# A two-matrix macaron block with an S4 convolution: the second half of the convolution by pairs of blocks, and a rewritten opening

## The chip, the cores and the metric

The kernel runs on one core of one Trainium2 chip. The metric is device time in microseconds for one launch. A NeuronCore has TensorE (PE; its weight loads are listed apart as PEld), VectorE (DVE), ScalarE (ACT), GpSimd (POOL) and SyncE (SP), which here only issues DMAs.

## The reference

The input `u` is 2 x 1024 x 1024 in float32. With LN a layer norm without weights, three residual steps follow each other:

```
x = u
x = x + 0.5 * FFN(LN(x))
x = x + S4(LN(x))
x = x + 0.5 * FFN(LN(x))          # the same weights as in the first FFN

FFN(x) = (silu(x @ Wg) * (x @ Wu)) @ Wd        # 1024 -> 2752 -> 1024
W[k, n] = scales[k // 128, n] * (w4[k, n] - (z4[k // 128, n] + 1))   # 4 bits, packed by 8 in int32

S4(u):  K = ifft of a rational function of 64 poles at 1024 roots of unity
        y = irfft(rfft(u, 2048) * rfft(K, 2048))[..., :1024]      # causal convolution along the last axis
        return y + D * u
```

The convolution runs along the last axis, 1024 long, and is the same for each of the 2048 rows. It is therefore a product with a Toeplitz matrix: output column m gets the sum over n <= m of u[n] K[m - n]. Cut into 8 x 8 blocks of 128, the block that takes input block c to output block m depends on m - c alone and is zero for m < c.

## The kernel before

**Tiling.** The 2048 rows are four token blocks of 512 (`TB`), each four tiles of 128 (`NT`). `JOBS` lists eight jobs (block, step): each is one feed-forward pass over one block, in the order (0,1), (1,1), (0,3), (1,3), (2,1), (3,1), (2,3), (3,3). Step 3 is the second FFN. A job has two stages, `gate_up` and `down`.

**gate_up** has 64 steps: eight waves of two or three pairs of 128 columns, and in each wave the eight groups of 128 input rows. In a step every unit of 128 columns gets two products of 512 columns, with the low and the high part of the normalized and turned input (`pieces`; L501). Between groups the partial sum in PSUM is multiplied by the ratio of two scales (`scaled`; L477 on ACT, L479 on DVE), so the weights themselves stay small integers. On the last group of a wave `gated` makes silu(gate) * up (L523, L526) and splits it into a high and a low part on GpSimd (L528, L530). `acc` has six PSUM banks for the six units. **down** has 44 steps, 22 for each half of the output, with products at L562 and the same rescales.

**Weights.** Job 0 also makes the weights. `fetch` and `fetch_zeros` load packed words and zero points, `split` separates even and odd nibbles (L381, L382), `dequantize` subtracts (L396) and writes the result to a DRAM buffer `w_q` (L400); `load_w` reads tiles back (L461), `AHEAD` = 3 steps early, from a pool of six buffers that `dequantize` shares. The first tile of all is put together in SBUF by eight small DMAs on ACT's queue (L399). `zero_points` makes the table of zero points and writes it to DRAM, from where `fetch_zeros` spreads it over partitions.

**Order.** The work around the matmuls hangs on steps: `at(up, s, f)` and `at(dn, s, f)` run `f` when step `s` of a stage is written. The program's framework then orders the instructions of each engine by when it expects them to be ready and, among ready ones, by the order of writing; so an instruction can come earlier on its engine than it was written. It also inserts the waits.

**The opening**, before the first step: zero points, loads of x, `moments` (bn_stats, L137) and `deviations` (1/sqrt by Newton steps on tiny tiles), `less_mean` (L1173), the eight `dequantize` of wave 0, the first scales, the multiplication by 1/deviation (L1185), and `turn` (transposes L173, high part L187, low part L188). Second halves of x are turned in steps 0 to 3.

**The convolution.** Between step 1 and step 3 of a block, in jobs 1, 2, 5 and 6, each of its four token tiles is normalized, turned (`turn_whole`; tile `st`) and convolved (`convolve`; products L835 into `pc`, adds L843). `toeplitz` holds the 8 different Toeplitz blocks, 128 x 1024, made in job 1 by `s4_tables`. `bank` hands out the two PSUM banks of the pool `ps`. The products are in float32: each shows as two matmul and two weight-load instructions.

Of the kernel before, what the change touches and what calls it, by code (L numbers as in the profile page):

```python
# [9 lines left out]
F32 = mybir.dt.float32  # L10
# [6 lines left out]
AX = mybir.AxisListType  # L17
PSUM = bass.MemoryType.PSUM
DRAM = bass.MemoryType.DRAM

P = 128
# [28 lines left out]
def macaron_s4_kernel(  # L50
# [64 lines left out]


# [52 lines left out]
    def turned(n, half, name, bank=bank):  # L169

        ps = bank(name)
        for k in range(4):
            nc.tensor.transpose(ps[:, bass.ts(k, P)], n[:, bass.ts(4 * half + k, P)], ident)  # L173
        return ps.rearrange("p (c t) -> p c t", c=4)
# [4 lines left out]
    def turn(b, t, n, half, bank=bank):  # L179
# [6 lines left out]
        ps = turned(n, half, f"pt_{b}_{k}_{t}_{half}", bank)  # L186
# [22 lines left out]
    def zero_points():  # L209

        n, nd = INTER // 8 // SEG, HID // 8 // SEGD
        z = t2("zq").bitcast(I32)[:, : n + nd]
        nc.gpsimd.memset(z, 0)
        for i, src in enumerate((gate_qz, up_qz)):
            own = slice(GK * SEG * i, GK * SEG * (i + 1))
            nc.scalar.dma_start(z[own, :n], src.rearrange("g (s n) -> (g s) n", s=SEG))
        nc.scalar.dma_start(z[: GD * SEGD, n:], down_qz.rearrange("g (s n) -> (g s) n", s=SEGD))
        zi = t4("zi").bitcast(I32)[:, : 8 * (n + nd)]
        for k in range(8):
# [8 lines left out]
        tab = t2("ztab").bitcast(BF16)[:, : 8 * (n + nd)]  # L228
        nc.vector.tensor_scalar(tab, zi, 1.0, None, ALU.add)
        nc.scalar.dma_start(z_dram.rearrange("g (s n) -> (g s) n", s=SEG), tab[:, : 8 * n])  # L230
        nc.scalar.dma_start(
            zd_dram.rearrange("g (s n) -> (g s) n", s=SEGD), tab[: GD * SEGD, 8 * n :]
        )
# [157 lines left out]
    def dequantize(w, j):  # L391
# [6 lines left out]
        if w == 0:  # L398
            nc.scalar.dma_start(first_tile[j:P:8].bitcast(F32), q[: P // 8].bitcast(F32))  # L399
# [34 lines left out]
    def first_weights(up, dn, at):  # L434


        for w in range(1, len(WAVES)):
            s0 = 8 * w - 12
            at(up, max(0, s0 - 3), lambda w=w: (fetch(w), fetch_zeros(w)))
            at(up, max(0, s0 - 1), lambda w=w: split(w))  # L440
            for j in range(8):
                s = s0 + j if w > 1 else (1, 2, 2, 3, 3, 3, 4, 4)[j]
# [11 lines left out]
    AHEAD = 3  # L454

# [25 lines left out]
    def gate_up(j, b, hooks):  # L481
        hi, lo = pieces[b]
        ps = {}
        ready = {s: load_w(j, s) for s in range(AHEAD)}
        for s, (wi, g) in enumerate(STEPS):
            if s + AHEAD < len(STEPS):
                ready[s + AHEAD] = load_w(j, s + AHEAD)
# [8 lines left out]
            for pos, (unit, col) in enumerate(order):  # L496
# [12 lines left out]
                if g < GK - 1:  # L509
                    on_act = unit % 2 == 0 or (j == 0 and pos == 1 and g % 4 < 3)  # L510
# [79 lines left out]
    toeplitz = const.tile([P, HID], F32, tag="toeplitz", name="toeplitz")  # L590
    k_dram = dpool.tile([1, P - 1 + HID], F32, tag="k", name="k_dram")
# [570 lines left out]
    for t, src in enumerate(rows_of(u, 0)):  # L1162
        nc.sync.dma_start(x[0][t], src)
        if t == 1:
            fetch(0)
# [110 lines left out]
```

## Time and profile before

| | |
|---|---|
| median of 3 runs | 2224.56 us (2221.06 to 2226.02) |
| the profiled execution | 2220.67 us, span 2218.9 us |
| PE busy | 2134.2 us, 96% |
| DVE busy | 1712.8 us, 77% |
| ACT busy | 1452.8 us, 65% |
| POOL busy | 328.8 us, 15% |
| DMA | 359.91 MB, mean 162 GB/s |
| first gate/up product starts | 35.44 us |
| convolution products, L835 | 384 instructions, 126.5 us busy |

The profile is one execution; times in it count from the start of its span. In a group's line the columns are: line, engine, operation, output <- input tiles, shapes and count, then busy time in us and mean ns of one, then the idle time of the engine just before these instructions and what ended most of it. Matmuls overlap their neighbours, so the distance between starts, not the duration of one, tells what a product costs.

### The profile page before, as it was taken

What the parts mean: (1) busy time and instruction counts of PE and PEld (TensorE: products, weight loads), DVE (VectorE), ACT (ScalarE), POOL (GpSimd) and SP (SyncE); (2) the same over time, 40 slices, a digit from 0 to 9 for tenths busy, and PEclk for the clock granted to TensorE, in tenths of its full rate; (3) what the DMA queues carried; (4) which work ended last, traced back from release to release, by engine and by line L of the source; (5) the groups of instructions that cost most, each with busy time, mean ns of one, the idle gap of its engine ahead of it and who ended that gap; (6) DMA issues with size and microseconds to landing.
All of it is one profiled execution on the core that took longest, in us unless ns stands there. A gap on an engine that the chain in (4) does not pass through costs nothing.

```text
span 2218.9 us, 28013 instructions
## 1 busy us (share of the span) xinstructions
PE 2134.2 (96%) x9364; PEld 1683.4 (76%) x9364; DVE 1712.8 (77%) x2792; ACT 1452.8 (65%) x2229; POOL 328.8 (15%) x350
## 2 busy tenths in 40 slices
PE   4898889999999999999999999999999999999998
PEld 3676667867887778888788878877788777888876
DVE  7898869767786878877887777867788677777776
ACT  5776776545764677677767777646676467767775
POOL 0232002211011230122102320102201023012210
PEclk9999999999999999999999999999999999999999
DMA  7788784434443545644455444434444354554444
GB/s 238 271 261 274 233 250 131 141 96 150 135 149 107 174 135 173 225 146 136 142 185 187 126 138 138 150 104 159 138 136 146 108 180 134 156 189 144 135 136 130
DMA packets 163667, 359.91 MB, mean 162 GB/s; under 512 B 22395, under 2 KB 27588, under 8 KB 163518
## 3 DMA queue, kind: packets, MB, share of 16 engines
q1 hardware_dynamic: 162730, 357.47, 51.8%
q8 instruction: 78, 1.28, 0.2%
q10 hardware_dynamic: 788, 0.58, 0.1%
q14 instruction: 71, 0.58, 0.1%
HBM read 306.86 MB, written 50.73 MB: 161 GB/s over the span
## 4 chain that ended last, share of the span: by engine, by line
PE 51%; issue 35%; DMA 5%; DVE 5%; POOL 3%; ACT 1%; SPq 0%; ACTq 0%; DVEq 0%; POOLq 0%
PE pg L501 35%; PE po L562 9%; PE pc L835 5%; POOL hl L530 2%; POOL hh L528 1%; DMA w<-wq 1%; DMA wd<-wdq 1%; DMA wdq<-qd 1%; DVE pg L479 1%; DVE hf L526 1%; DVE q L396 1%; PE st L173 1%; DMA wq<-q 1%; PE pt L173 0%; PE pb L583 0%
## 5 line engine op out<-in xcount | busy, mean ns | idle before, releaser
L477 ACT ACTIVATE pg<-pg,rat 128x512 f32<-128x512 f32 x1256 | 820.1, 662 | 467.0 <-PE pg L501 462.4
L501 PE MATMUL pg<-xTl,w 128*128 128x512 f32 x2752 | 1084.3, 396 | 27.9 <-DVE pg L479 12.2
L501 PE MATMUL pg<-xTh,w 128*128 128x512 f32 x2752 | 1070.9, 391 | 0.0
L479 DVE TENSOR_TENSOR pg<-pg,rat 128x512 f32<-128x512 f32 x1152 | 785.8, 696 | 162.9 <-PE pg L501 154.1
L501 PEld LDWEIGHTS pg<-xTl,w 128*128 128x128 f32 x2752 | 517.8, 188 | 164.1 <-DVE pg L479 22.6
L501 PEld LDWEIGHTS pg<-xTh,w 128*128 128x128 f32 x2752 | 518.6, 188 | 103.3 <-issue 0.2
L562 PE MATMUL po<-hl,wd 128*128 128x512 f32 x1344 | 538.2, 403 | 18.4 <-DVE po L479 7.7
L477 ACT ACTIVATE po<-po,ratd 128x512 f32<-128x512 f32 x670 | 438.7, 662 | 170.1 <-PE po L562 169.8
L562 PE MATMUL po<-hh,wd 128*128 128x512 f32 x1344 | 521.3, 392 | 0.0
L479 DVE TENSOR_TENSOR po<-po,ratd 128x512 f32<-128x512 f32 x610 | 419.1, 697 | 93.5 <-PE po L562 89.2
L528 POOL CAST hh<-hf 128x512 fp32r<-128x512 f32 x168 | 109.4, 651 | 1755.1 <-DVE hf L526 1630.5
L562 PEld LDWEIGHTS po<-hl,wd 128*128 128x128 f32 x1344 | 252.1, 188 | 96.4 <-DVE po L479 18.4
L562 PEld LDWEIGHTS po<-hh,wd 128*128 128x128 f32 x1344 | 253.4, 189 | 46.0
L530 POOL TENSOR_TENSOR hl<-hf,hh 128x512 fp32r<-128x512 f32 x168 | 222.9, 1327 | 13.5
L526 DVE SCALAR_TENSOR_TENSOR hf<-pg,rat,g 128x512 f32<-128x512 f32 x168 | 125.1, 748 | 78.6 <-PE pg L501 32.6
L523 ACT ACTIVATE g<-pg,rat 128x512 f32<-128x512 f32 x168 | 115.6, 689 | 41.8 <-PE pg L501 39.2
L835 PE MATMUL pc<-toeplitz,st 128*128 128x512 f32 (+3 forms) x384 | 126.5, 486 | 0.0
L835 PEld LDWEIGHTS pc<-toeplitz,st 128*128 128x128 f32 x384 | 70.3, 190 | 57.4 <-issue 46.0
L843 DVE TENSOR_TENSOR x<-x,pc 128x512 f32<-128x512 f32 x32 | 22.0, 686 | 77.4 <-PE pc L835 77.2
L137 DVE BATCH_NORM_STATS2 stats<-x 128x6 f32<-128x512 f32 x96 | 64.6, 679 | 2.2 <-DMA x<-in_L_attn_u_dram 1.1
L188 DVE TENSOR_TENSOR xTl<-pt,xTh 128x512 fp32r<-128x512 f32 x64 | 43.5, 685 | 17.3 <-ACT xTh L187 17.3
L173 PE MATMUL pt<-ident,xn 128*128 128x128 f32 x256 | 42.9, 286 | 14.1 <-ACT xn L1185 14.1
(135 smaller groups left out, 617.5 us busy)
## 6 DMA issues: line engine op xcount, KB each, us to landing
w<-wq SPq DMA_DIRECT2D x319, 384.0 KB
wd<-wdq SPq DMA_DIRECT2D x336, 256.0 KB
w<-wq SPq DMA_DIRECT2D x128, 256.0 KB
w<-wq SPq DMA_DIRECT2D x64, 320.0 KB
x<-in_L_attn_u_dram SPq DMA_DIRECT2D x32, 512.0 KB
wq<-q SPq DMA_DIRECT2D x40, 384.0 KB
wdq<-qd SPq DMA_DIRECT2D x32, 256.0 KB
xs<-x SPq DMA_DIRECT2D x16, 512.0 KB
```

The lines of the kernel that those rows point to most:

```text
L137: nc.vector.bn_stats(stats[:, t, i, :], x[b][t][:, bass.ts(i, 512)])
L173: nc.tensor.transpose(ps[:, bass.ts(k, P)], n[:, bass.ts(4 * half + k, P)], ident)
L188: nc.vector.tensor_tensor(lo, ps, hi.bitcast(F32), ALU.subtract)
L477: nc.scalar.activation(dst, src, AF.Copy, scale=sc)
L479: nc.vector.tensor_tensor(dst, src, sc.to_broadcast([P, TB]), ALU.mult)
L501: nc.tensor.matmul(p, w[:, bass.ts(col, P)], part[:, g, :], start=(g == 0 and k == 0), stop=(g == GK - 1 and k == 1), skip_group_check=True,)
L523: nc.scalar.activation(g, pg, AF.Silu, scale=rat[:, 2 * f, GK - 1 :])
L526: nc.vector.scalar_tensor_tensor(hf, pu, last, g, ALU.mult, ALU.mult)
L528: nc.gpsimd.tensor_copy(hi, hf)
L530: nc.gpsimd.tensor_tensor(lo, hf, hi.bitcast(F32), ALU.subtract)
L562: nc.tensor.matmul(ps[c], w[:, bass.ts(c, P)], part, start=(f == 0 and k == 0), stop=(f == NF - 1), skip_group_check=True,)
L835: nc.tensor.matmul(ps[:, lo - 512 * nh :], lhsT(c), toeplitz[:, lo - P * c : end - P * c], start=(c == 0), stop=(c == last),)
```

## The change

Three parts; the core of the diff follows.

1. **Convolution.** The second half of the output (blocks 4 to 7) is computed by pairs. With inputs a (even block) and b (odd block), and T1, T2, T3 the Toeplitz blocks at three neighbouring distances, a pair of outputs needs a T2 + b T1 and a T3 + b T2. These are (a + b) T2 + b (T1 - T2) and (a + b) T2 + a (T3 - T2): three products for four. The sums a + b are made on GpSimd, the differences `ahead` and `after` once in job 1. `own` and `both` are two PSUM banks; `both` is added twice, to each block of a pair.
2. **Opening.** The x tiles are loaded by SP and ACT, two each; the zero points of `down` are made later and apart; the packed words of wave 1 are fetched earlier; x is normalized in halves of 512 columns; the first tile's DMAs go to GpSimd's queue; and `in_order_of_writing` ties the instructions of ACT, DVE and SP to the order in which they are written.
3. **Job 0 and 1.** In job 0 the second unit's rescale is always on ACT (before: three steps of four), weight tiles are loaded two steps ahead, scales come in other portions at other steps, raw fetches and splits keep the order of writing, and the moments and the normalizing of the next block come later in `down`. In job 1 the pieces of the S4 tables keep the order of writing.

```diff
+    def in_order_of_writing(f, *engines):
+        start = len(nc.cur_bb.bb.instructions)
+        f()
+        written = list(nc.cur_bb.bb.instructions)
+        for e in engines:
+            last = next((i for i in reversed(written[:start]) if i.engine == e), None)
+            for ins in written[start:]:
+                if ins.engine == e:
+                    if last is not None:
+                        tc.add_manual_dep(ins, last.name, ...)
+                    last = ins
...
-            nc.scalar.dma_start(first_tile[j:P:8].bitcast(F32), q[: P // 8].bitcast(F32))
+            nc.gpsimd.dma_start(first_tile[j:P:8].bitcast(F32), q[: P // 8].bitcast(F32))
...
         for w in range(1, len(WAVES)):
             s0 = 8 * w - 12
-            at(up, max(0, s0 - 3), lambda w=w: (fetch(w), fetch_zeros(w)))
-            at(up, max(0, s0 - 1), lambda w=w: split(w))
+            if w > 1:
+                both = lambda w=w: (fetch(w), fetch_zeros(w))
+                at(up, s0 - 3, lambda both=both: in_order_of_writing(both, ET.SP))
+                at(up, s0 - 1, lambda w=w: in_order_of_writing(lambda: split(w), ET.DVE))
+            else:
+                at(up, 0, lambda: in_order_of_writing(lambda: split(1), *STARTING))
             for j in range(8):
-                s = s0 + j if w > 1 else (1, 2, 2, 3, 3, 3, 4, 4)[j]
+                s = s0 + j if w > 1 else (1, 2, 2, 3, 3, 4, 4, 5)[j]
...
     AHEAD = 3
+    FIRST = 2
...
-        ready = {s: load_w(j, s) for s in range(AHEAD)}
+        ahead = AHEAD if j else FIRST
+        ready = {s: load_w(j, s) for s in range(ahead)}
...
-                    on_act = unit % 2 == 0 or (j == 0 and pos == 1 and g % 4 < 3)
+                    on_act = unit % 2 == 0 or (j == 0 and pos == 1)
...
+        for dst, d in ((after, 3), (ahead, 1)):
+            nc.vector.tensor_tensor(dst, blocks[:, d : d + 5 : 2], blocks[:, 2:7:2], ALU.subtract)
...
+    def convolve(b, t, s, name):
+        ps = bank(f"pc_{name}_0")
+        for c in range(4):
+            nc.tensor.matmul(ps[:, P * c :], s[:, c, :], toeplitz[:, : 512 - P * c],
+                start=(c == 0), stop=(c == 3))
+        part = x[b][t][:, :512]
+        nc.vector.tensor_tensor(part, part, ps, ALU.add)
+
+        sums = ypool.tile([P, TB], F32, tag="y", name=f"sums_{name}")
+        sums = sums[:, : 3 * P].rearrange("p (c t) -> p c t", c=3)
+        nc.gpsimd.tensor_tensor(sums, s[:, 0:6:2, :], s[:, 1:6:2, :], ALU.add)
+        own = bank(f"pc_{name}_1")
+        both = bank(f"pc_{name}_2")[:, : 2 * P].rearrange("p (y m) -> p y m", y=2)
+        flat = own.rearrange("p (y m) -> p y m", y=4)
+        upper, lower = flat[:, 0:4:2], flat[:, 1:4:2]
...
+        for y in range(2):
+            product(flat[:, 2 * y : 2 * y + 2], s[:, 4 + 2 * y, :], blocks[:, 0:2], start=(y == 0))
+        for y in range(2):
+            product(flat[:, 2 * y + 1], s[:, 5 + 2 * y, :], blocks[:, 0])
+        for i in range(3):
+            y = slice(max(0, i - 1), 2)
+            d = slice(max(0, 1 - i), 3 - i)
+            product(lower[:, y], s[:, 2 * i, :], after[:, d])
+            product(upper[:, y], s[:, 2 * i + 1, :], ahead[:, d], stop=(i == 2))
+        for i in range(3):
+            y = slice(max(0, i - 1), 2)
+            d = slice(2 * max(1, 2 - i), 2 * (3 - i) + 1, 2)
+            product(both[:, y], sums[:, i, :], blocks[:, d], start=(i == 0), stop=(i == 2))
+        part = x[b][t][:, 512:]
+        nc.vector.tensor_tensor(part, part, own, ALU.add)
+        part = part.rearrange("p (y h m) -> p y h m", y=2, h=2)
+        twice = both.unsqueeze(2).to_broadcast([P, 2, 2, P])
+        nc.vector.tensor_tensor(part, part, twice, ALU.add)
...
-                for s, k0, k1 in ((2, 3, 11), (12, 11, 19), (20, 19, WIDE)):
+                for s, k0, k1 in ((4, 3, 9), (20, 9, 15), (36, 15, WIDE)):
...
-                at(up, 28, scales_down)
+                at(up, 40, scales_down)
                 for t in range(NT):
-                    at(up, t, lambda t=t: turn(0, t, first[t], 1))
+                    at(up, t, lambda t=t: in_order_of_writing(lambda: second_half(t), *STARTING))
...
                 for s in range(2, 42):
-                    at(up, s, lambda: next(tables, None))
+                    piece = lambda: next(tables, None)
+                    at(up, s, lambda: in_order_of_writing(piece, ET.DVE, ET.Activation))
...
-                    stage, o = (dn, 0) if j == 0 else (up, 44)
-                    at(stage, o, lambda: moments(ab, 1))
+                    stage, o = (dn, 14) if j == 0 else (up, 44)
+                    at(stage, o, lambda: in_order_of_writing(lambda: moments(ab, 1), ET.DVE))
...
-                o = 3 if j == 0 else 0
+                o = 20 if j == 0 else 0
...
+    STARTING = ET.Activation, ET.DVE, ET.SP
...
+    def less_mean(t, half):
+        first[t, half] = t2(f"xn_0_1_{t}_{half}")
+        src = x[0][t][:, bass.ts(half, 512)]
+        nc.scalar.activation(first[t, half], src, AF.Identity, bias=means[t], scale=-1.0)
+
+    def by_deviation(t, half):
+        n = first[t, half]
+        nc.scalar.activation(n, n, AF.Copy, scale=ln[0, t][1])
+
+    def second_half(t):
+        by_deviation(t, 1)
+        turn(0, t, first[t, 1], 1)
+
+    def start():
+        zeros = zero_words(0)
+        x[0] = [t4(f"x_0_{t}") for t in range(NT)]
+        for t, src in enumerate(rows_of(u, 0)):
+            (nc.sync, nc.scalar)[t // 2].dma_start(x[0][t], src)
+        fetch(0)
+        srow = scale_rows(0, 3)
+        zeros_down = zero_words(1)
+        fetch(1)
+        zero_points(0, zeros)
+        fetch_zeros(0)
+        fetch_zeros(1)
+
+        def then(t, m):
+            means[t] = m
+            less_mean(t, 0)
+            if t == 2:
+                split(0)
+
+        moments(0, 1, then)
+        deviations(0, 1, -1.0)
+        for i in range(8):
+            dequantize(0, i)
+        for t in range(NT + 1):
+            if t < NT:
+                by_deviation(t, 0)
+            if t:
+                turn(0, t - 1, first[t - 1, 0], 0, acc)
+        for t in range(NT):
+            less_mean(t, 1)
+        scales(0, 3, srow)
+        zero_points(1, zeros_down)
+
+    in_order_of_writing(start, *STARTING)
```

## The prediction

> **What bounds the kernel now.** I read the page's table of engines and its slices first, then the costliest groups, then the busy time in stretches cut at the kernel's stages, and last the timeline around one convolution and of the opening.
>
> ```profile
> PE 2134.2 (96%) x9364; PEld 1683.4 (76%) x9364; DVE 1712.8 (77%) x2792; ACT 1452.8 (65%) x2229; POOL 328.8 (15%) x350
> PE   4898889999999999999999999999999999999998
> ...
> L835 PE MATMUL pc<-toeplitz,st 128*128 128x512 f32 (+3 forms) x384 | 126.5, 486 | 0.0
> L843 DVE TENSOR_TENSOR x<-x,pc 128x512 f32<-128x512 f32 x32 | 22.0, 686 | 77.4 <-PE pc L835 77.2
> ```
>
> TensorE is the bound from slice 7 on (nines); only slices 1 to 6, the opening and job 0, have room. The convolution never waits (idle 0.0), and VectorE waits 77.2 us for it.
>
> ```profile
> 223.60:328.40 104.80, 92.11 (x394) 68.10 (x393) 80.12 (x164) 76.26 (x125) 3.89 (x4) 0.98 0.76 239
> 1403.70:1598.40 194.70, 193.77 (x834) 150.69 (x833) 143.61 (x242) 117.17 (x178) 35.29 (x38) 1.00 0.44 137
> 911.60:1071.60 160.00, 159.48 (x706) 130.25 (x706) 123.13 (x182) 114.95 (x174) 35.42 (x38) 1.00 0.53 166
> 35.40:223.60 188.20, 171.53 (x723) 129.23 (x723) 161.54 (x249) 140.27 (x223) 46.00 (x38) 0.99 0.80 267
> ```
>
> These are, in columns: length, busy PE, PEld, DVE, ACT, POOL, clock, DMA share, GB/s. Job 3's gate/up stage (third row, no convolution) lasts 160.0 us and is all TensorE. Job 5's (second row, four convolutions) lasts 194.7 and is all TensorE too: 34.7 more for convolutions and their transposes, with no bubble. Job 0's gate/up (fourth) needs 188.2 for the 160's work, with DVE at 86% and DMA at 80%; its down stage (first) takes 104.8 where job 1's takes 86.1.
>
> ```profile
> 462.74 7.91 PE L835 MATMUL pc<-toeplitz,st 128*128 128x512 f32 x24
> 465.09 0.69 DVE L843 TENSOR_TENSOR x<-x,pc 128x512 f32<-128x512 f32 x1 [1.46 <-PE pc L835]
> 470.40 0.48 PE L501 MATMUL pg<-xTl,w 128*128 128x512 f32 x1
> 470.68 0.69 DVE L843 TENSOR_TENSOR x<-x,pc 128x512 f32<-128x512 f32 x1 [4.18 <-PE pc L835]
> ```
>
> One convolution: 24 instructions (12 products, two each) from 462.74 to 470.40, 7.66 us in one piece; VectorE stands idle 1.46 and 4.18 us inside it.
>
> ```profile
> 16.35 0.96 DVE L396 TENSOR_TENSOR q<-even,z 128x768 fp32r<-128x768 uint8 x1 [1.73 <-DMA z<-z_dram]
> 17.34 10.04 ACTq L399 DMA_DIRECT2D w<-q  x8
> 27.48 3.23 ACT L1185 ACTIVATE xn<-xn,r 128x1024 f32<-128x1024 f32 x3 [11.42 <-DMA w<-q]
> 31.09 1.76 SPq L461 DMA_DIRECT2D w<-wq  x4
> 35.44 0.50 PE L501 MATMUL pg<-xTl,w 128*128 128x512 f32 x1 [1.40 <-DVE xTl L188]
> ```
>
> The opening: ScalarE sits 11.42 us behind eight DMA issues (27.48), so normalizing, transposing and splitting come after the weights, and the first product starts at 35.44.
>
> **What the Trainium skill says.** "TensorE: Matmul & The Clock Gate", LDWEIGHTS: a weight load takes its columns over 1.2 ns, 107 ns for 128. Here 4,608 columns took 7.66 us, 1.662 ns a column with thin products included, so a 128-column instruction (213 ns a product, 107 each) just covers its load; the trace agrees. "DMA: Bandwidth & Descriptors", Issuing engines are not separate DMA queues: moving x tiles to ACT's queue saves issue time alone; no run here shows the opposite. The same page, Latency: first byte about 1 us from GpSimd's queue, 0.6 from SP's and ACT's. "SBUF — State Buffer", two separate sides: GpSimd can be locked out of writing descriptors while VectorE holds the shared port. No DMA from GpSimd is in the trace of before.
>
> **The convolution.** Before, a token tile's products have 512+384+256+128 columns for the first half and 4x512+1,280 for the second: 4,608. After: the first half's 1,280; then own blocks 256+256+128+128 = 768; two sets of difference products 256+256+128 = 640 each; the common ones 640. That is 3,968 in 17 products. Saved: 640 x 1.662 = 1.064 us per tile, 16 tiles: **17.0 us**. Ten more weight loads per tile (34 for 24) lie under products of 107 ns or more each, so I cost them at nothing; bound: each of the twelve thin instructions (six 128-column products, two each) shows 0.02 us of it, 16 x 12 x 0.02 = 3.8 us.
>
> Added on VectorE: one add of 512 columns from PSUM per tile, 0.69 by L843's row, 16 x 0.69 = 11 us. The add of `own` now falls while TensorE does the 640 common columns (1.06 us), so only one add remains after the end, as before. VectorE is 74% busy in job 5's stage; cost nothing. If that cover failed, at most 11 us. Added on GpSimd: a sum of 384 columns, 1.0 us by L530's 1,327 ns per 512. `both` needs it 3.4 us + 2.1 us after the convolution's start; the copies of s it reads end earlier still (458 and 459.7 for the product at 462.7). Behind a burst of three hh/hl pairs (2 us each) it could be late by 1 us; I expect it ahead of them. A third PSUM bank per tile takes the one of `pc_0`, whose add ends 3.0 us into it, well before 5.5. Two table subtractions, about 0.5 us each once, in job 1. I take 16.5 of 17.0.
>
> **The opening.** VectorE does zero points (0.4 us less without the down part, which goes behind), moments and split as one run: from about 6.1, 1.2 + 5.7 + 1.1 + 0.5 us, then ten tiny steps of about 0.17; r is ready near 16.3, not 25.6. z still needs its two round trips (8.24 to 12.36 to 16.35 before); `z_dram` is written 0.8 us earlier but behind two x tiles on ACT's queue and, on SP's, behind raw_1 (0.79 MB, 2.7 us at 290 GB/s). I take no change: dequantizing starts at 16.4, runs 8 x 0.87 without the tiny steps between, ends at 23.4 (before 24.3). Meanwhile ScalarE, free of DMA issues, turns x (eight instructions of 0.6). The first tile comes by GpSimd's queue: 1 us for each of eight, the last at 26 to 31 if the port is held. `wq0` and first tile are 3.5 MB; at the 297 GB/s of 20 to 30 us they land at 29.5; then w_0_1 (issue 31.09 before, behind z_1 and raw_2) lands near 32.6. Step 1 therefore starts at 32.6 where it started at 38.3 (13th product): **5.7 us** earlier. SP is passed by srow, the down zeros and raw_1, all ahead of fetch_zeros(0); POOL by eight DMAs that replace ACT's.
>
> **Job 0 after that.** The second unit's rescale goes to ScalarE in the fourth step too: eight of 0.62, 5.0 us off VectorE (161.5 of 188.2 busy), onto ScalarE (140.3 of 188.2). Of the stalls only part is VectorE's, so I take half, 2.5. Only two weight tiles ahead instead of three: a tile has 2 x 2.72 = 5.4 us to land instead of 8.2; loads took 3.6 (125.02) to 6.45 (75.42) on the chain. I take +2.0, from 0 to +8. `second_half` adds 4 x 0.6 us on ScalarE in steps 0 to 3, which has 0.3 to spare each; in the 2.0. Raw fetches and splits kept in order of writing, moments moved from the end of gate/up (202 to 212; TensorE was busy 7.6 us of 200 to 210) to down step 14, normalizing later by 17 steps: 0, from -6 to +6; the burst of 7 us on VectorE at step 14 holds up the fourth rescale and the products behind it, against relief earlier. Job 1's table pieces in order: 0, from -2 to +3.
>
> Sum: -16.5 - 5.7 - 2.5 + 2.0 = -22.7 against the profiled execution's 2220.67 (span 2218.9): **2198.0**. The median shown, 2224.56, is 3.9 higher than that execution, within the spread of 5 us.
>
> **Rivals.** (a) The convolution alone pays: TensorE starts earlier but job 0 is held to the pace of its 50 MB (188.2 x 267 GB/s) and VectorE, so the start is only waited away. For: DMA 0.80, DVE 0.86. Against: neither is full. 2220.7 - 16.5 = 2204. (b) Job 0 comes loose: moments away from its tail, a third buffer for q, VectorE relieved. Its 28 us above 160 and 18.7 above 86.1 are the prize; a third, 13 more, gives 2185. (c) **Slower**: w tiles come late because only two are under way while wq writes fill the DMA. TensorE then waits for landing time less 5.4 us on each of 62 loads. If all took 6.45, +63 us less the 22.7 above, near 2260; it decides from 5.4 + 22.7/62 = 5.8 us on. Against it: before lost only 7.0 us to w in all. (d) The pairing doesn't save what it says: TensorE waits 1 us for the sum on each tile, or thin products cost their loads; with an opening that gives nothing, 2220.
>
> **Numbers.** The named forecast (2192 to 2201): 0.45. (a), 2201 to 2214: 0.27. (b), 2178 to 2192: 0.18. (c): 0.06. (d): 0.04. About 0.2% (4.4 us) is what a measurement of this kernel can tell from no change. Faster is the first three, 0.90; the same (d), 0.04; slower (c), 0.06. The range 2180 to 2214 leaves out (c), (d) and the far end of (b).
>
> **What would show it.** One convolution lasts 6.6 us in one piece, idle 0.0 before its products, in all 16 places; job 5's gate/up lasts 190.5. The first gate/up product starts by 30 and the 13th near 32.6. ACT shows no wait on w<-q. Job 0's gate/up and down together stay under 291 us. Wrong: PE waiting on POOL for `sums`, on DVE for `pc`'s bank, a convolution above 7.1 us, or a w<-wq wait well over 7.0 us in job 0.

## The result, and the profile after

The kernel after takes 2221.08 us (median of 4 runs, 2217.81 to 2223.84), the kernel before, run beside it, 2222.81 (4 runs). The ratio is 0.9992, with a 95% interval of 0.997 to 1.0014: no difference that can be told. The forecast was 2198, faster, so it was wrong. The profiled execution took 2223.84 us (span 2222.0), 3.2 us more than that of before. It lies 2.8 us above its kernel's median, that of before 2.1 us below, so the two profiles stand about 5 us further apart than the medians.

The page of after, its table of engines, slices and costliest group:

```profile
PE 2129.5 (96%) x9524; PEld 1708.8 (77%) x9524; DVE 1719.0 (77%) x2811; ACT 1455.9 (66%) x2245; POOL 345.4 (16%) x373
PE   5897899999999999999999999999999999999998
...
L534 PE MATMUL pg<-xTl,w 128*128 128x512 f32 x2752 | 1086.4, 398 | 40.6 <-DMA w<-wq 19.1
```

and the same group of before:

```profile
L501 PE MATMUL pg<-xTl,w 128*128 128x512 f32 x2752 | 1084.3, 396 | 27.9 <-DVE pg L479 12.2 <-DMA w<-wq 7.0 <-DVE hf L526 4.7
```

L534 is the line of the gate/up products (L501 before). The busy totals hardly moved. What moved is the idle time ahead of these products: 40.6 us, of which 19.1 ended with the landing of a weight tile; before it was 27.9 us, and 7.0 of that for w.

The busy time in stretches, cut at the same stages as before (length; busy PE, PEld, DVE, ACT, POOL with their counts; clock, DMA share, GB/s): job 0's gate/up and down, then the gate/up of jobs 1, 3 and 5.

```profile
30.70:231.60 200.90, 175.71 (x728) 135.39 (x729) 148.37 (x229) 146.34 (x235) 42.95 (x38) 0.96 0.80 258
231.60:340.00 108.40, 95.32 (x393) 69.64 (x392) 81.84 (x144) 74.57 (x123) 4.43 (x4) 0.95 0.72 231
340.00:553.90 213.90, 207.89 (x926) 165.00 (x925) 170.49 (x339) 118.19 (x182) 40.95 (x46) 0.98 0.42 128
918.90:1080.70 161.80, 160.89 (x706) 129.67 (x705) 129.75 (x206) 114.04 (x174) 35.94 (x39) 1.00 0.54 164
1415.00:1605.60 190.60, 189.67 (x874) 155.87 (x873) 146.48 (x247) 117.17 (x178) 39.42 (x43) 1.00 0.46 140
```

Read against before: job 0 starts 4.8 us earlier (30.7 for 35.4), yet its gate/up needs 200.9 for 188.2 and it ends at 340.0 where before ended at 328.3. Job 5, with four convolutions, needs 190.6 for 194.7: the convolution pays 4.1 to 4.2 us there, as forecast. Job 3, which has no convolution, became longer, 161.8 for 160.0 (job 4: 162.9 for 159.9), and job 1 won only 0.8 (213.9 for 214.7) with its four convolutions.

One convolution in the timeline of after:

```profile
477.67 1.00 POOL L885 TENSOR_TENSOR sums<-st 128x384 f32<-128x384 f32 x1
477.82 2.32 PE L873 MATMUL pc<-toeplitz,st 128*128 128x512 f32 x8
...
483.45 1.25 PE L892 MATMUL pc<-toeplitz,sums 128*128 128x256 f32 x6
483.66 0.69 DVE L908 TENSOR_TENSOR x<-x,pc 128x512 f32<-128x512 f32 x1 [2.07 <-PE pc L892]
...
484.46 0.48 PE L534 MATMUL pg<-xTl,w 128*128 128x512 f32 x1
```

It lasts from 477.82 to 484.46, 6.64 us for 7.66. GpSimd's sums (1.00 us) are there 4.8 us before the product that reads them, and VectorE's added add (L908) falls inside the products. Fifteen of the sixteen convolutions take 6.64 us; one, at 731.7, takes 7.82, with the run's one wait of TensorE for a PSUM bank.

The opening, in the timeline of after:

```profile
16.48 0.96 DVE L423 TENSOR_TENSOR q<-even,z 128x768 fp32r<-128x768 uint8 x1
...
25.25 0.48 POOL L426 DMA_DIRECT2D w<-q  x1 [1.19 <-DVE q L423]
...
30.68 0.77 PE L534 MATMUL pg<-xTl,w 128*128 128x512 f32 x1 [3.77 <-DMA w<-q]
31.25 0.63 PE L534 MATMUL pg<-xTh,w 128*128 128x512 f32 x1
```

Dequantizing starts at 16.48 (forecast 16.4), but the last eighth of the first tile is issued at 25.25 and the first product waits for it until 30.68. Its successors come at the slow spacing of 0.43 us until 34.2, and the 13th product (step 1) starts at 35.70; before it was 38.29, the forecast 32.6.

Last, where TensorE and SP stood in job 0 (waits of PE over the whole run; then TensorE and SP's queue in the timeline). "SPq" is a DMA issued by SP.

```profile
PE pg L534 <- DMA w<-wq: 19.1, 10, 4.7
```

```profile
64.20 0.77 PE L534 MATMUL pg<-xTl,w 128*128 128x512 f32 x1 [3.90 <-DMA w<-wq]
...
203.44 0.77 PE L534 MATMUL pg<-xTl,w 128*128 128x512 f32 x1 [4.70 <-DMA w<-wq]
204.00 0.63 PE L534 MATMUL pg<-xTh,w 128*128 128x512 f32 x1
204.43 0.63 PE L534 MATMUL pg<-xTl,w 128*128 128x512 f32 x1
...
209.11 0.40 PE L534 MATMUL pg<-xTl,w 128*128 128x512 f32 x1
209.35 0.39 PE L534 MATMUL pg<-xTh,w 128*128 128x512 f32 x1
```

```profile
193.17 0.42 SPq L436 DMA_DIRECT2D rawd<-_L_ffn_down_qweight_dram  x1
193.64 0.61 SPq L441 DMA_DIRECT2D zd<-zd_dram  x1
194.30 1.06 SPq L145 DMA_DIRECT2D x<-in_L_attn_u_dram  x2
199.85 0.33 SPq L457 DMA_DIRECT2D wdq<-qd  x1
200.27 0.38 SPq L493 DMA_DIRECT2D w<-wq  x1
```

```profile
198.33 0.43 DVE L408 TENSOR_SCALAR rawd<-rawd 128x512 int32<-128x512 int32 x1 [1.32 <-DMA rawd<-_L_ffn_down_qweight_dram]
198.79 0.43 DVE L409 TENSOR_SCALAR rawd<-rawd 128x512 int32<-128x512 int32 x1
199.14 0.68 DVE L455 TENSOR_TENSOR qd<-rawd,zd 128x512 fp32r<-128x512 uint8 x1
```

The three fences are one chain. The packed words of down (`rawd`) are issued at 193.17, where before issued them at 164.43. VectorE waits for them until 198.33 and has the first `qd` at 199.8. SP's next entry is the write of that `qd`, so SP stands from 195.4 to 199.85, with the load of a weight tile behind it in the same queue. TensorE waits 4.70 us for this tile. After the wait TensorE is slow: products come every 0.43 us until 208.3, every 0.23 after. The wait at 64.20 is another: `w_0_8` needs all eight `wq` writes of wave 1, and wave 1's dequantizing ended at 58.7 (before: 56.5). A third wait for a weight tile, of 3.53 us, comes at 220.79.

### The profile page after: what moved, and what is told of

It reads as the page before. It is cut to its first block, busy times and chain, and to the rows that moved or that the text cites. A ratio compares the mean times of both kernels' runs of the same rounds, so it can differ in the third digit from the quotient of the medians.

```text
span 2222.0 us, 28395 instructions
## 1 busy us (share of the span) xinstructions
PE 2129.5 (96%) x9524; PEld 1708.8 (77%) x9524; DVE 1719.0 (77%) x2811; ACT 1455.9 (66%) x2245; POOL 345.4 (16%) x373
## 4 chain that ended last, share of the span: by engine, by line
PE 64%; issue 23%; DVE 5%; POOL 3%; DMA 3%; ACT 1%; SPq 0%; ACTq 0%; DVEq 0%; POOLq 0%
PE pg L534 41%; PE po L595 17%; PE pc L892 3%; POOL hl L563 2%; PE pc L873 1%; POOL hh L561 1%; DMA wd<-wdq 1%; DVE pg L511 1%; DMA w<-wq 1%; PE pb L616 1%; DVE hf L559 1%; PE st L194 1%; PE pt L194 1%; DVE q L423 1%; DMA w<-q 0%
## 5 line engine op out<-in xcount | busy, mean ns | idle before, releaser
L534 PE MATMUL pg<-xTl,w 128*128 128x512 f32 x2752 | 1086.4, 398 | 40.6 <-DMA w<-wq 19.1
L534 PE MATMUL pg<-xTh,w 128*128 128x512 f32 x2752 | 1071.3, 393 | 0.0
L534 PEld LDWEIGHTS pg<-xTl,w 128*128 128x128 f32 x2752 | 519.6, 189 | 181.8 <-DVE pg L511 18.2
L534 PEld LDWEIGHTS pg<-xTh,w 128*128 128x128 f32 x2752 | 520.9, 189 | 103.6 <-issue 0.2
L208 ACT CAST xTh<-pt 128x512 fp32r<-128x512 f32 x64 | 37.7, 589 | 22.8 <-PE pt L194 22.7
L194 PEld LDWEIGHTS pt<-ident,xn 128*128 128x128 f32 x256 | 33.8, 149 | 23.7 <-ACT xn L1239 12.6
L618 DVE TENSOR_TENSOR x<-x,pb 128x512 f32<-128x512 f32 x64 | 43.2, 677 | 0.6 <-PE pb L616 0.6
```

What stands on the lines that cost most here:

```text
L194: nc.tensor.transpose(ps[:, bass.ts(k, P)], n[:, bass.ts(k, P)], ident)
L534: nc.tensor.matmul(p, w[:, bass.ts(col, P)], part[:, g, :], start=(g == 0 and k == 0), stop=(g == GK - 1 and k == 1), skip_group_check=True,)
```

## The experiments

All ratios are to the kernel before, run beside, with 95% intervals. The stage table at the end of this section holds one profiled execution each.

**Which half loses?** The change was cut in two.

e1_conv_only, before with the new convolution and nothing else:

```diff
 before.py
-    def convolve(b, t, src, name):        # 12 products
+    def convolve(b, t, s, name):          # 17 products, sums, own, both, as in after
```

> The kernel before with nothing but the new convolution (three products for four, GpSimd's sums, the second add, the two difference tables). Theory 'convolution pays, job 0 loses': the four stages with convolutions each last 4.2 us less, everything else is as before, so 2222.8 - 17 = 2206, ratio 0.9925; no new wait on POOL or on the third bank. Rival 'what the convolution saves is given back elsewhere' (clock, VectorE, banks): 2219 or more, ratio 0.998 to 1.002.

Measured: 2208.70 us, 0.9936 (0.9923 to 0.995). The convolution alone is worth 14.2 us; jobs 2, 5 and 6 are 3.2 to 4.2 us shorter each, job 1 by 3.1.

e2_opening_only, after with the old convolution:

```diff
 after.py
-    def convolve(b, t, s, name):          # 17 products
+    def convolve(b, t, src, name):        # 12 products, as in before
```

> The changed kernel with the old convolution: the opening, rescales, lookahead, order of writing and moved moments alone. Theory: the start is 4.8 us earlier, but job 0 loses 12.9 us in gate/up and 5.8 in down and jobs 1, 3 and 4 about 3, 1.8 and 2.9, so 2222.8 + 18 = 2241, ratio 1.008 (1.005 to 1.010). Rival 'the opening is neutral': 2219 to 2227, ratio within 0.002 of 1.

Measured: 2234.37 us, 1.0053 (1.004 to 1.0067). The rest of the change costs 11.8 us; 18 were expected. Both halves together, -0.0064 and +0.0053, give the -0.0008 of the whole change within its interval. So the forecast convolution is there, and the opening with the orders of job 0 and 1 takes it back.

**Two tiles ahead, or the moments?**

e3_three_ahead:

```diff
 after.py
-                s = s0 + j if w > 1 else (1, 2, 2, 3, 3, 4, 4, 5)[j]
+                s = s0 + j if w > 1 else (1, 2, 2, 3, 3, 3, 4, 4)[j]
-    FIRST = 2
+    FIRST = 3
```

> The changed kernel with weight tiles three steps ahead in job 0 too, and wave 1's dequantizing at the steps of before (three at a time in step 3, the last in step 4), which three ahead needs. Theory 'two ahead is too late': the waits of TensorE for w tiles in job 0 fall from 19.0 us to about 7, and with them the slow clock behind each long one; job 0's gate/up from 201 to about 190, total 2210. Rival 'the pinned order and the moved moments make the tiles late': the waits stay above 15 us, 2219 to 2223.

Measured: 2223.25 us, 1.0008 (1.0001 to 1.0016). The wait at step 8 is gone (its first product at 59.4 for 64.2), waits for w fall from 19.1 to 13.0 us, and the time doesn't fall: others come, one of 3.6 us for ScalarE at 116, and job 0 still ends at 336.5. The theory that the two tiles ahead are the loss fell.

e4_moments_free, the moments of the next block not tied to the order of writing and at `down` step 0 again, normalizing from step 4 on:

```diff
 after.py
-                    stage, o = (dn, 14) if j == 0 else (up, 44)
-                    at(stage, o, lambda: in_order_of_writing(lambda: moments(ab, 1), ET.DVE))
+                    stage, o = (dn, 0) if j == 0 else (up, 44)
+                    at(stage, o, lambda: moments(ab, 1))
-                o = 20 if j == 0 else 0
+                o = 3 if j == 0 else 0
```

> The changed kernel with the next block's moments not tied to the order of writing, in job 0 at down step 0 again, and normalizing at down steps 4 to 16 again. Theory: jobs 3 and 4 come back to 160.0 us in gate/up (4.7 us less in all), job 0's down comes back from 108.6 to about 103; w waits in gate/up stay near 19 us: total 2211. Rival 'these moves are neutral, the 160s differ by the clock alone': 2219 to 2223, jobs 3 and 4 still near 162.

Measured: 2211.41 us, 0.9956 (0.9942 to 0.997), 9.7 us less than after by the medians, 8.0 by the ratios. Its stretches, job 0's two stages and job 3's gate/up:

```profile
29.80:227.20 197.40, 174.87 (x728) 135.07 (x729) 155.57 (x251) 146.12 (x235) 43.08 (x38) 0.97 0.81 263
227.10:330.30 103.20, 94.02 (x394) 70.27 (x392) 75.16 (x125) 74.78 (x123) 4.21 (x4) 0.95 0.75 238
909.90:1070.00 160.10, 159.57 (x706) 130.34 (x705) 123.22 (x183) 114.90 (x174) 35.52 (x39) 1.00 0.54 167
```

Job 0's down is back from 108.4 to 103.2 and job 3 from 161.8 to 160.1. Untied, the moments run long before the step at which they are written, and spread out: in e4 bn_stats of job 0 from 198 to 218 us, those written in job 3 between 838 and 940. Tied, they run as one burst on VectorE, in job 0 of after from 270.5 to 277.5; in job 3 they fill 1039.5 to 1047 but for one rescale between two pairs, and TensorE's products between 1036 and 1056 lose about 1.5 us to waits and wider spacing, those of e4 in the same part of job 3 none. Why job 0's gate/up is also 3.5 us shorter in e4 is not shown.

e5_three_and_free, e3's edit and e4's together:

```diff
 e4_moments_free
+    FIRST = 3                             # and wave 1's steps as in e3_three_ahead
```

> The changed kernel with both: three weight tiles ahead (wave 1's steps as before) and the moments free. Theory 'the late tile of step 8 is repaired by three ahead, the rest of the loss is the moments': the stall of 4.1 us at step 8 (64 us) is gone, job 0's gate/up ends by 224, total 2206. Theory 'pace': job 0's making of weights sets when it ends, whatever the start and the lookahead; it ends at 227 again with other stalls, total 2211, as with the moments free alone.

Measured: 2213.93 us, 0.9961 (0.9947 to 0.9976). Against e3 the freed moments give 9.3 us here too. Job 0 ends at 332.6, e4's at 330.2. A tile more under way brings nothing here either.

**What sets job 0's pace: VectorE or the transfers?** From e4, two doses of one suspect each.

e6_fewer_rescales leaves out job 0's rescale of the fourth unit (31 us of VectorE's work):

```diff
 e4_moments_free
-                    scaled(on_act, p, p, rat[:, unit, g : g + 1])
+                    if j or pos != 3:
+                        scaled(on_act, p, p, rat[:, unit, g : g + 1])
```

> Moments free, and in job 0 the fourth unit of a step is not rescaled (left out: about 35 to 40 us of VectorE's work in job 0's gate/up; the output of job 0 is not the reference's). If VectorE sets job 0's pace: gate/up falls from 197.5 to 175 to 185 us, total 2190 to 2199. If the DMA sets it: no more than 3 us less, 2208 to 2212.

e7_half_read loads only the first half of each weight tile's columns in job 0 and uses it for both halves, so 11.3 MB fewer are read; every product is still made:

```diff
 e4_moments_free
-        nc.sync.dma_start(t.bitcast(F32), w_q[w][bass.ts(g, P), :])
+        part = len(WAVES[w]) * P if j == 0 else width_of(w)
+        nc.sync.dma_start(t[:, :part].bitcast(F32), w_q[w][bass.ts(g, P), :part])
...
-                        w[:, bass.ts(col, P)],
+                        w[:, bass.ts(col % n if j == 0 else col, P)],
```

> Moments free, and job 0 loads only the gate half of each weight tile and multiplies the up units by it too (left out: half of job 0's reads of w, about 11 of 52 MB; job 0's output is not the reference's). If the DMA sets job 0's pace: the w waits fall under 5 us and gate/up from 197.5 to 178 to 188, total 2192 to 2202. If VectorE sets it: gate/up stays above 193, 2207 to 2212.

Measured: e6 2211.48 us, 0.9947 (0.9929 to 0.9965); e7 2196.76 us, 0.9886 (0.9871 to 0.9901). Job 0's gate/up of e6, then of e7:

```profile
30.60:225.80 195.20, 172.02 (x727) 133.97 (x727) 124.35 (x198) 146.50 (x236) 44.19 (x39) 0.97 0.81 263
```

```profile
30.30:213.00 182.70, 171.01 (x728) 131.93 (x729) 159.47 (x256) 145.69 (x235) 43.68 (x38) 0.99 0.68 222
```

VectorE 20% less busy (155.6 to 124.4): the stage is 2.2 us shorter and the time does not move. DMA share 0.81 to 0.68: 14.7 us shorter, waits for w down from 16.8 to 5.7 us. So the transfers set the pace of job 0's gate/up, and VectorE, in this order of work, does not.

e11_conv_half_read, the same cut made in e1_conv_only, that is, with the old opening:

```diff
 e1_conv_only
+        # the edit of e7_half_read
```

> The kernel before with the new convolution, and in job 0 only the gate half of each weight tile loaded and used for the up units as well (left out: half of job 0's reads of w; job 0's output is not the reference's). If the DMA paces job 0 with the old opening too: gate/up falls from 191.9 by 8 to 14 us, total 2195 to 2201. If the old order of work was limited by VectorE instead: less than 3 us, 2206 to 2209.

Measured: 2191.84 us, 0.9857 (0.9842 to 0.9872). Job 0's gate/up of e1, then of e11:

```profile
35.50:227.40 191.90, 174.13 (x723) 131.61 (x723) 162.07 (x249) 140.07 (x223) 45.80 (x38) 0.97 0.79 261
36.30:213.60 177.30, 170.05 (x724) 131.60 (x725) 160.94 (x263) 139.53 (x223) 43.37 (x39) 0.98 0.67 222
```

About the same 14.7 us (`down` starts at 213.4, in the last stretch), and no wait on w<-wq is left, where e1 has 8.1 us of them: the pace was there before the change. With the old order no run took work off VectorE.

**Is the earlier start worth anything?** e8_start_alone has the convolution and the new opening, and jobs 0 and 1 as before, except that the second halves of x and the split of wave 1, in steps 0 to 3, stay tied:

```diff
 e5_three_and_free
-  fetch, fetch_zeros, split, table pieces: in_order_of_writing
+  fetch, fetch_zeros, split, table pieces: untied
-                    on_act = unit % 2 == 0 or (j == 0 and pos == 1)
+                    on_act = unit % 2 == 0 or (j == 0 and pos == 1 and g % 4 < 3)
-                for s, k0, k1 in ((4, 3, 9), (20, 9, 15), (36, 15, WIDE)):
-                at(up, 40, scales_down)
+                for s, k0, k1 in ((2, 3, 11), (12, 11, 19), (20, 19, WIDE)):
+                at(up, 28, scales_down)
```

> The new convolution and the new opening before step 0, with everything in job 0 after that as before: three tiles ahead, wave 1's steps, rescales, portions of scales, fetches and splits not tied, moments free, table pieces not tied. Theory 'the pinned order and the moved work in job 0 cost the gain of the start': job 0 as long as before and 4.8 us earlier, so 2208.7 - 4.8 = 2204. Theory 'pace': the earlier start is waited away in job 0 and it comes out at the convolution alone, 2207 to 2211.

Measured: 2210.16 us, 0.9948 (0.9934 to 0.9961). The first product comes at 30.6 for e1's 35.5, and job 0 ends at 335.8 for e1's 331.6 (in an execution 3.5 us above e8's median). The earlier start alone wins nothing.

**The x tiles at the tail.** e10_x_later loads the next block's x in `down` instead of beside the last weight tiles:

```diff
 e4_moments_free
-                    at(up, 55 if j == 0 else 6, lambda: load_x(ab, rows_of(u, ab)))
-                    stage, o = (dn, 0) if j == 0 else (up, 44)
+                    at(dn if j == 0 else up, 2 if j == 0 else 6, lambda: load_x(ab, rows_of(u, ab)))
+                    stage, o = (dn, 12) if j == 0 else (up, 44)
-                o = 3 if j == 0 else 0
+                o = 20 if j == 0 else 0
```

> Moments free, but the next block's four x tiles (2 MB) are loaded at down step 2 of job 0 instead of gate/up step 55, the moments come at down step 12 and normalizing at steps 21 to 33. Theory 'x stands in front of the weight tiles': the stall of 6.4 us at 202 us is gone and gate/up falls from 197.5 to 191 to 193; but the 2 MB (7 us at 290 GB/s) then compete in down, so the two stages together (300.8) come out at 296 to 300, total 2207 to 2211. Rival 'SP waits there for VectorE's down weights anyway': gate/up stays at 196 to 198.

Measured: 2210.09 us, 0.9947 (0.9933 to 0.996), against e4's 0.9956: not told apart. Job 0's gate/up is 192.6 for 197.5, but the wait near 203 us is still there (4.65 us, at 200.8). Its moments are written two steps before the place that they have in after, and its normalizing just where after has it, but nothing is tied: they run from 219 to 238, and the time is e4's. So the tie, and not the later place, is what costs in after; x moved as well here, so this is not a clean pair.

**The late words.** The wait near 203 us was over 4.6 us in every kernel that issued `rawd` at 190 to 193 (after, e2, e4, e6, e10), and at most 2.5 us in the full kernels where it went out at 163 to 181. e12_words_early moves that one fetch in after; e13_fetch_free unties the fetches and splits that delay it.

```diff
 after.py
-                at(*when(max(0, n - 3)), lambda a=a, rt=rt: fetch_down(a, rt))
+                at(*(when(max(0, n - 3)) if n else (up, 44)), lambda a=a, rt=rt: fetch_down(a, rt))
```

> The kernel after, with one line moved: the packed words of down's first part (rawd of (0,0)) are fetched at step 44 of job 0's gate/up instead of step 52. Everything else as in after. In after those words are issued at 193.17, VectorE waits 1.32 us for them at 198.33, SP sits until 199.85 for the qd made of them, and the w load behind it ends a wait of TensorE of 4.70 us at 203.44, with ten slow products after it (2 us). Theory 'queue': the late words block SP's queue; rawd is issued near 175, the wait at 203 us shrinks to under 2.5, and most of 6.7 us stays won: job 0's down ends near 334, time 2215 (ratio 0.9965 to 0.998). Theory 'pace': the wait goes, but the weights of job 0 need their time anyway and the w loads wait elsewhere: down ends at 338 to 342, time 2219 to 2223 (ratio 0.999 to 1.001). Rival: something else of SP's queue is late there, the wait stays at over 4 us.

```diff
 after.py
-                at(up, s0 - 3, lambda both=both: in_order_of_writing(both, ET.SP))
-                at(up, s0 - 1, lambda w=w: in_order_of_writing(lambda: split(w), ET.DVE))
+                at(up, s0 - 3, lambda both=both: both())
+                at(up, s0 - 1, lambda w=w: split(w))
```

> The kernel after without the two ties in job 0's gate/up: fetch and fetch_zeros of waves 2 to 7 not tied on SP, split not tied on VectorE. Moments, two tiles ahead, rescales and scales as in after. Theory 'ties': the tied fetches are what puts down's first words at 193 (before and the kernels without these ties issued them at 164 to 171); rawd comes near 170, no w wait of over 3 us near 203, gate/up lasts 192 to 195 instead of 201, time 2212 to 2215 (ratio 0.996 to 0.997). Theory 'pace': gate/up 197 to 201, time 2218 to 2222 (ratio 0.998 to 1.0).

Measured: e12 2216.40 us, 0.9974 (0.9963 to 0.9985); e13 2218.93 us, 0.9986 (0.9979 to 0.9994). The words go out at 174.3 and 163.3, and the wait at 203 is gone in both. In the timeline of e12:

```profile
200.30 0.50 PE L534 MATMUL pg<-xTl,w 128*128 128x512 f32 x1 [0.81 <-DMA w<-wq]
209.66 0.77 PE L534 MATMUL pg<-xTl,w 128*128 128x512 f32 x1 [4.50 <-DMA w<-wq]
```

So the late words cost 4.0 us by the ratios, 4.7 by the medians (2221.08 less 2216.40; the two intervals overlap), although a new wait of 4.5 us appears 9 us later; e13 and e14 have one of 3.5 and 3.6 us there too. Untying the fetches and splits moves the words as well, shortens gate/up to 195.2 and still wins only 1 to 2 us, within the interval of after.

**Do the losses add up, and is the start then kept?** First the other half of the convolution. e9_both_halves is e1 with the first half by pairs too (own blocks and two difference products, a third column block in `both`, 3,840 columns for 3,968):

```diff
 e1_conv_only
-        for c in range(4):
-            nc.tensor.matmul(ps[:, P * c :], s[:, c, :], toeplitz[:, : 512 - P * c], ...)
+        product(front[:, 3], s[:, 0, :], after[:, 0])      # beside the blocks' own products
+        product(front[:, 2], s[:, 1, :], ahead[:, 0], stop=True)
...
-            product(both[:, y], sums[:, i, :], blocks[:, d], start=(i == 0), stop=(i == 2))
+            product(both[:, i:3], sums[:, i, :], blocks[:, d], start=(i == 0), stop=(i == 2))
...
-        twice = both.unsqueeze(2).to_broadcast([P, 2, 2, P])
+        twice = both.unsqueeze(2).to_broadcast([P, 3, 2, P])
```

> The kernel before with the convolution by pairs in both halves: the first half's blocks 2 and 3 also by three products for four, which saves 128 columns more per token tile, and one second add of 768 columns instead of 512. At 1.662 ns a column, 16 x 128 x 1.662 = 3.4 us less than the pairs in the second half alone; each of the four stages 0.85 us shorter (189.8 for 190.7). Total 2208.7 - 3.4 = 2205, ratio to before 0.992. Rival: the common product, which now has to be there for the first half too, and the longer add hold up what follows: 2208 to 2212.

Measured: 2205.74 us, 0.9922 (0.9908 to 0.9935), jobs 5 and 6 at 190.0 each for 190.7. The stages show the gain; the two totals, 3.0 us apart, are not told apart.

e14_together is after with e4's, e12's and e9's edits and untied table pieces:

```diff
 e4_moments_free
+  down's first words at step 44, both halves by pairs
-                    at(up, s, lambda: in_order_of_writing(piece, ET.DVE, ET.Activation))
+                    at(up, s, piece)
```

> The kernel after with four edits together: moments free and written at down step 0 (as in e4_moments_free), down's first words at step 44 (as in e12_words_early), both halves of the convolution by pairs (as in e9_both_halves), the pieces of the S4 tables not tied. If the causes add up ('sum'): 2221.1 less 9.7 (moments) less 4.7 (words) less 3 (pieces) less 3 (first half) = 2200.7, ratio 0.989 to 0.992, and job 0's down ends near 325, under every kernel that read all its weights (328.2 to 340.0). If the weights' transfers hold job 0 ('pace'): its down ends at 328 to 332 as in the others, time 2204 to 2207, ratio 0.992 to 0.994.

Measured: 2203.55 us, 0.9915 (0.9899 to 0.9931), the fastest of the kernels that do all the work. The ratio lies in the range of "sum"; job 0's end, 328.2, is that of "pace", in an execution 2.9 us below the median. It starts 5.5 us ahead of before and ends job 0 at the same time. And e9, the same convolution with the start and the order of before, is at 0.9922: with everything mended, the rest of the change is not told apart from nothing.

The stage table (us; the first gate/up product, the end of job 0's down, and from there to the last product of down):

| kernel | first product | job 0 ends | the rest |
|---|---|---|---|
| before | 35.4 | 328.3 | 1878.5 |
| after | 30.7 | 340.0 | 1869.7 |
| e1 convolution | 35.5 | 331.6 | 1863.9 |
| e2 opening | 30.4 | 335.7 | 1885.5 |
| e3 three ahead | 30.5 | 336.5 | 1870.7 |
| e4 moments free | 29.8 | 330.2 | 1866.6 |
| e5 both of these | 30.4 | 332.6 | 1866.7 |
| e6 fewer rescales | 30.7 | 329.8 | 1866.6 |
| e7 half read | 30.3 | 314.8 | 1866.9 |
| e8 start alone | 30.6 | 335.8 | 1863.2 |
| e9 both halves | 36.8 | 330.9 | 1857.9 |
| e10 x later | 31.1 | 328.2 | 1867.1 |
| e11 e1, half read | 36.3 | 315.9 | 1863.0 |
| e12 words early | 30.1 | 330.6 | 1869.9 |
| e13 fetch free | 31.2 | 333.8 | 1871.4 |
| e14 together | 29.9 | 328.2 | 1857.8 |

Only the two kernels that read less end job 0 before 328. A row is one execution, and that need not be a median one: after and e8 lie 2.8 and 3.5 us above their medians, before, e9, e12 and e14 1.8 to 2.9 us below.

## Why the prediction was wrong

**The convolution: right.** 16.5 us were forecast, e1 gained 14.2 (11 to 17 by its interval) and the stages without job 0 gained 14.6. The 1.662 ns a column held for thin products (6.64 us for 3,968 columns is 1.67), and the covers that were named held: GpSimd's sums hidden, VectorE's second add inside the products, one wait of 0.9 us for a PSUM bank in the whole run. That wait and the one convolution of 7.82 us are signs of being wrong that the prediction had named, but they cost 1.2 us.

**The opening: its times right up to the first tile.** 1/deviation was ready at 16.6 us (16.3), dequantizing started at 16.48 (16.4); it ended at 24.95 (23.4), as VectorE waited 0.71 us for the landing of one of the first tile's DMAs. GpSimd's eight issues took 0.48 to 0.65 us each, for 1 us in the sum, with no sign of the locked-out port that the bound allowed for. But the landing was put at 29.5 and its reader started at 30.68, and the sum left out that TensorE is slow after a long wait: step 1 started at 35.70 instead of 32.6. Of 5.7 us, 2.6 were there.

**The failed step: the credit of the earlier start (5.7) and of VectorE's relief (2.5) in job 0.** The prediction read 86% of VectorE and 80% of DMA as "neither is full" and gave rival (a), the pace of the 50 MB, 0.27. e7 and e11 show that the transfers set that pace, at a share of 0.79 to 0.81. e6 took 31 us of work off VectorE, six times the 5.0 that the change was to take off, and won nothing. Job 0's two stages, which were to stay under 291 us, took 309.3. The earlier start is worth nothing that can be told: 0.9948 with it (e8) and 0.9936 without (e1), 0.9915 with everything mended (e14) and 0.9922 without (e9). That it is waited away on the transfers is inferred from two things. Dequantizing, from which the weights come, starts no earlier (16.48 for 16.35). And the lead over before, 4.2 to 5.7 us at the first product, is gone at step 12, at 73 to 80 us: there the full kernels with the new opening stand between 1.5 us ahead (e3) and 5.0 us behind (e8). The Trainium skill, "DMA: Bandwidth & Descriptors", Specifications, gives about 358 GB/s as a core's limit to HBM; job 0's gate/up ran at 256 to 268 GB/s of mixed reads and writes in the kernels that read all their weights, and was held by them, so the figure is no measure of the room left here.

**The term put at nothing.** Tied fetches and splits, moved and tied moments and later normalizing stood together at 0 (-6 to +6). The text named the burst of 7 us on VectorE and set it off against relief earlier; the runs show the burst and no relief. Freeing the moments gave 9.7 us by the medians and 8.0 by the ratios; in the profiled executions job 0 ends 9.8 earlier and the rest is 3.1 shorter. That jobs 3 and 4 are touched at all was not seen: the tie also holds where the step (`up`, 44) did not move. The late words are some 4 us more (e12, with overlapping intervals): a wait at the head of SP's queue that the text, which listed what SP is passed by, didn't follow to the loads queued behind.

**The smaller terms.** Two tiles ahead stood at +2.0 (to +8); three ahead gave nothing back (e3, e5). Job 1's pieces stood at 0 (-2 to +3): job 1 takes 213.9 tied and 210.8 (e8) to 211.6 (e1) untied, 2 to 3 us; no run frees them alone.

The account of the profiled executions closes: job 0 was to end at 328.3 - 6.2 = 322.1 and ended at 340.0, 17.9 later; the rest was to take 1878.5 - 16.5 = 1862.0 and took 1869.7, 7.7 more. Together 25.6 of the 25.8 us between the forecast sum and the execution. By the medians the change brought 1.7 us instead of 22.7. The causes, added up, give 22.5 to 25.9 us for these 21.0: 8.2 of credits, 8.0 to 9.7 of moments, 4.0 to 4.7 of words, 2 to 3 of pieces and 2.3 of the convolution, less the 2.0 set aside. This sum is an estimate; the parts need not be independent.

**The rivals.** (a) had the mechanism. Its 2204 was not reached with this convolution (e1 2208.7, e8 2210.2); e14 and e9 come near it with 128 columns fewer per token tile. And it too priced the tied work at nothing. (c), tiles late because only two are under way, fell with e3: its waits came, 19.1 us for 7.0, but with three ahead 13.0 stayed, and the time with them. (b) and (d) did not happen.

**Open.** e8, with before's order and an earlier start, ends job 0 4 to 6 us later than e1 and e4; its execution was slow by 3.5 us, and whether anything remains is not settled. Nor is why e13, with the words earliest of all full kernels, gains no more than e12. Three kernels with before's order of job 0 and its start (before, e1, e9) end it at 328.3 to 331.6, so differences of 3 us in that column of the table carry nothing.

## What to carry to other kernels

Before crediting an earlier start, ask whether the stage behind it is paced by something that starts no earlier; halve that something's volume in one run and see if the stage shortens. A busy share of 80% on DMA can already be the pace, as in job 0 here. And a tie to the order of writing costs where it makes a burst on an engine that others wait for, or puts a write that must wait at the head of a queue of loads; price it at every place where the tied code runs, also where nothing was moved.

## What the runs showed of the hardware

TensorE's products come at half speed after some waits. In after, behind waits of 3.77, 3.90 and 4.70 us, they start every 0.43 us for 3.5 to 4.9 us, then every 0.23; the clock column of job 0's gate/up reads 0.96, 0.99 before. The length of the wait alone does not decide it. Behind 2.34 and 2.84 us in e1 (at 104.34 and 213.58) they were slow for 3.1 us; behind 2.26, 2.40 and 2.65 us in e3 (204.13, 78.59, 64.58) not at all; behind 3.53 us in after (220.79) only 1.5 us later. The Trainium skill, "TensorE: Matmul & The Clock Gate", Part 1: The HAM clock gate, states that an idle window of about 3.4 us halves the clock and that about 3.4 us of work restores it. The halved speed and roughly the length of the recovery agree with the trace; a wait of 2.34 us is shorter than that window, and there the trace decides. The page calls the penalty under 1% of a span. That holds: in job 0's gate/up of after 33 products came 0.38 to 0.48 us after the one before, 6.6 us lost, 0.3% of the span (10 and 2.1 us before). But it is about as much as the start was to win. One stretch of eight to eleven slow products costs 1.6 to 2.2 us beyond the wait.

Small DMAs landed late in the opening: the eight of the first tile (49 KB each), issued by GpSimd while `wq0` was being written, took 3.5 to 5.3 us from issue to landing. From 20 to 25 us the DMA share was 0.97, at 299 GB/s; no run shows these DMAs without that load.
